# Layer 2's frequency products with the spectra stationary, its weights put in order of use by copies in memory, and layer 1 woven

## The chip, the cores and the metric

One core of a Trainium2 chip runs the whole program. The metric is the device time of one execution in microseconds (us), as the median of several; a smaller number is better. Next to the times stands the profile of one execution, which names the engines: PE (TensorE matmuls), PEld (its loads of stationary operands), DVE (VectorE), ACT (ScalarE), POOL (GpSimd) and SP, the engine whose queue (SPq) issues most transfers. PEclk is the share of full clock that TensorE was granted. "Issue" as the cause of idle time means that the engine waited for nothing that the profile shows. "The chain" is the work that ended last, followed back from each step to what released it. A matmul leaves two records in these traces (8448 for the 4224 of the products below).

## The reference

Four layers in float32 on x of 2 x 128 x 64 x 64, each of the form x = x + layer(group_norm(x)):

```python
# layer 0: 1x1 convolution to 5*128 channels, depth-wise 3x3, two attentions (4 heads), projection
# layer 1: a 1x3 convolution, correlations over 7 shifts, a 5x5 dilated depth-wise convolution
# layer 2: quaternion convolution by FFT
Xs = rfft2(x in 4 groups of 32 channels)                       # 64 x 33 frequencies
Ws = kr_{w,x,y,z} + 1j * ki_{w,x,y,z}                          # each 32 x 32 x 64 x 33
C  = einsum('piohw,qbihw->pqbohw', Ws, Xs)                     # 4 x 4 products per frequency
Pw = C[0,0] - C[1,1] - C[2,2] - C[3,3]                         # ... Px, Py, Pz: other signs and pairs
o  = irfft2(P)
# layer 3: attention with 8 heads of 16 channels over 4096 tokens
```

Each of the 64 x 33 frequencies of layer 2 has its own 128 x 32 complex matrix of weights (69 MB in all), and it meets only 2 images. This is what makes layer 2 awkward: many small products, each with weights of its own.

## The kernel before

Layers 0 and 3 (attention) are the long ones and stay almost as they are. Layer 2 has a way in (normalize, transform over h), the products with the transform over w (8 blocks of 4 rows and their 4 mirror rows, so 16 half blocks), and a way out. Its loads and products, and the order of steps in layer 1:

```python
wpool = ctx.enter_context(tc.tile_pool(name="l2_w", bufs=5))
def rows_of_weights(kb, mirror):          # one half block: 4 rows of 33 frequencies
    for part in "ri":
        wt = wpool.tile([128, 32, NF], F32, tag="w", name=f"w_{part}")
        for p in range(4):                # runs of 4 * 33 values, 528 bytes, in DRAM
            ...
            nc.sync.dma_start(wt[32 * p : 32 * p + 32, :, at:],
                array[:, :, r0 : lo + 4, :].rearrange("i o h w -> i o (h w)"))
# spectra of one row: a matmul against a sign-and-place matrix, then the transform over w
def transposed(i):
    nc.tensor.matmul(pt, y[:, b, m, :, :]..., k["perm"], start=True, stop=True)   # 512 columns
    nc.scalar.copy(yt, pt)
def transformed(i, yt):
    for r in range(0, 4, 2): ...          # 4 matmuls of 198 columns a row and image, DVE copies to e
def products(ws, e, got):
    for fw in range(FW):                  # 33 frequencies
        for n in range(2):                # real and imaginary weights
            for s in range(4):            # 4 rows, one column group of PE each
                nc.tensor.matmul(out...,  # stationary: weights, 128 x 32; moving: 16 columns
                    ws[n][:, :, s * FW + fw],
                    e[:, s, :, :, 1 - n : 3 - n, fw]..., start=(n == 0), stop=(n == 1))
# layer 1
g = [padded(0)]; prepared(); g.append(padded(1))
xt = [columns(g[0])]; t2 = [convolved(g[0])]; xt.append(columns(g[1]))
t3 = [correlated(xt[0])]; t2.append(convolved(g[1])); t3.append(correlated(xt[1]))
some(taps(0, g[0]), 42)                   # DVE: 42 taps of the depth-wise convolution, image 0
```

## Time and profile before

| | before |
|---|---|
| median of 3 runs (a fourth came with the result) | 4674.4 us (4664.9 to 4683.0) |
| profiled span, granted clock | 4670.5 us, 0.932 |
| layer 0 ends at | 1687.1 us |
| layer 1 | 302.8 us |
| layer 2: way in, products, way out | 45.2, 539.9, 78.9 us |
| layer 3: first to last exp | 1946.5 us |

### The profile page before, as it was taken

The numbers are of one execution on the slowest core, as the hardware profiler recorded it, in microseconds if no ns is written. First come the engines' busy times: TensorE is split into PE (matmuls) and PEld (weight loads), VectorE is DVE, ScalarE is ACT, GpSimd is POOL, SyncE is SP. The second block draws the span as 40 slices with busy tenths as digits, with TensorE's granted clock in tenths as the row PEclk, the third lists the DMA queues.
The fourth block names the chain that finished last, engine by engine and source line by source line (L and its number), as shares of the span: only waits on it lengthen the run. The fifth ranks groups of instructions, "written<-read, shape, count | busy, mean of one in ns | idle before, by whom it ended". The sixth has DMA issues, their size and how long they took to land.

```text
span 4670.5 us, 95822 instructions
## 1 busy us (share of the span) xinstructions
PE 4291.4 (92%) x42698; PEld 1787.4 (38%) x42698; DVE 2118.5 (45%) x2192; ACT 3264.9 (70%) x3735; POOL 59.3 (1%) x141
## 2 busy tenths in 40 slices
PE   6899999889999968976677889999999999999998
PEld 3522222452222234465556733333333333333332
DVE  3689999458999986951111221131113211221111
ACT  3478888437888821221111289999999999999998
POOL 1001000000000010000000000000000000000000
PEclk9999999999999979986676589999999999999999
DMA  1000000000000000088876000000000000000000
GB/s 44 2 1 1 1 1 1 1 2 1 1 1 1 1 6 1 1 136 130 129 119 95 7 3 6 6 5 4 6 6 6 6 6 6 6 6 6 6 6 4
DMA packets 154267, 90.60 MB, mean 19 GB/s; under 512 B 24297, under 2 KB 148201, under 8 KB 153842
## 3 DMA queue, kind: packets, MB, share of 16 engines
q1 hardware_dynamic: 153842, 84.36, 11.1%
q8 instruction: 337, 5.52, 0.5%
q14 instruction: 88, 0.72, 0.1%
HBM read 75.94 MB, written 4.19 MB: 17 GB/s over the span
## 4 chain that ended last, share of the span: by engine, by line
PE 85%; DVE 6%; issue 4%; ACT 3%; POOL 1%; DMA 0%; SPq 0%; DVEq 0%; ACTq 0%; POOLq 0%
PE ps_acc L1884 22%; PE ps_s L1865 18%; PE ps_s L1166 12%; PE ps_acc L1570 11%; PE ps_sp L1361 3%; PE ps_freq L875 3%; PE ps_bank L673 2%; PE ps_pe L842 2%; PE ps_bank L819 1%; DVE sums L1605 1%; PE ps_t L605 1%; PE ps_sp L1339 1%; PE ps_po L994 1%; PE ps_bank L590 1%; PE ps_bank L644 1%
## 5 line engine op out<-in xcount | busy, mean ns | idle before, releaser
L1875 ACT ACTIVATE weights<-ps_s 128x1024 f32<-128x1024 f32 x2048 | 1887.6, 1094 | 60.0 <-PE ps_s L1865 57.3
L1175 ACT ACTIVATE weights<-ps_s 128x1024 f32<-128x1024 f32 x1024 | 992.7, 1022 | 176.4 <-PE ps_s L1166 151.5
L1884 PE MATMUL ps_acc<-weights,vt 128*32 128x512 f32 x8192 | 1092.1, 605 | 0.0
L1865 PE MATMUL ps_s<-q,k 32*128 32x512 f32 x8192 | 931.3, 445 | 10.3 <-ACT weights L1875 10.3
L1605 DVE TENSOR_TENSOR sums<-sums,weights 128x2048 f32<-128x2048 f32 x384 | 879.1, 2289 | 44.6 <-ACT weights L1175 8.8
L1865 PEld LDWEIGHTS ps_s<-q,k 32*128 32x128 f32 x8192 | 473.2, 182 | 847.7 <-ACT weights L1875 788.8
L1166 PE MATMUL ps_s<-q,k 32*128 32x512 f32 x4096 | 648.1, 643 | 2.7 <-ACT weights L1175 1.3
L1570 PE MATMUL ps_acc<-weights,vt 128*32 128x512 f32 x4096 | 550.3, 607 | 3.4 <-ACT used L1595 3.2
L1906 DVE COPY u<-ps_acc 128x512 f32<-128x512 f32 x32 | 22.1, 692 | 1067.4 <-PE ps_acc L1884 1067.4
L1166 PEld LDWEIGHTS ps_s<-q,k 32*128 32x128 f32 x4096 | 210.1, 184 | 431.2 <-issue 215.4
L1884 PEld LDWEIGHTS ps_acc<-weights,vt 128*32 128x32 f32 x8192 | 163.0, 108 | 378.0 <-issue 366.0
L1570 PEld LDWEIGHTS ps_acc<-weights,vt 128*32 128x32 f32 x4096 | 81.1, 108 | 396.6 <-issue 378.4
L875 PE MATMUL ps_freq<-e,w_i 128*32 128x16 f32 x4224 | 141.1, 220 | 72.6 <-issue 72.6
L875 PE MATMUL ps_freq<-e,w_r 128*32 128x16 f32 x4224 | 143.1, 220 | 68.0 <-issue 67.5
L625 DVE SCALAR_TENSOR_TENSOR X<-g,w,X 128x2048 f32<-128x2048 f32 x84 | 197.3, 2350 | 2.4
L1361 PE MATMUL ps_sp<-pad,diag 32*32 32x512 f32 x4608 | 168.3, 611 | 6.1 <-DVE q L1372 4.8
L1605 DVE TENSOR_TENSOR sums<-weights 128x2048 f32<-128x2048 f32 x64 | 146.5, 2289 | 60.6 <-ACT weights L1175 60.6
L875 PEld LDWEIGHTS ps_freq<-e,w_i 128*32 128x32 f32 x4224 | 134.0, 159 | 76.6 <-issue 76.5
L875 PEld LDWEIGHTS ps_freq<-e,w_r 128*32 128x32 f32 x4224 | 134.7, 159 | 74.6 <-issue 73.6
L885 ACT COPY pz<-ps_freq 128x272 f32<-128x272 f32 x16 | 6.8, 423 | 211.2 <-PE ps_freq L875 211.2
L1826 DVE TENSOR_TENSOR vt<-ps_acc,bv 128x384 f32<-128x384 f32 x32 | 17.8, 557 | 292.1 <-PE ps_acc L1819 292.1
L885 DVE COPY pz<-ps_freq 128x256 f32<-128x256 f32 x16 | 6.8, 425 | 278.3 <-PE ps_freq L875 208.7
(278 smaller groups left out, 3196.9 us busy)
## 6 DMA issues: line engine op xcount, KB each, us to landing
w_r<-in_L_conv_kr_w SPq DMA_DIRECT2D x15, 528.0 KB, 12.3
w_r<-in_L_conv_kr_x SPq DMA_DIRECT2D x15, 528.0 KB
w_r<-in_L_conv_kr_y SPq DMA_DIRECT2D x15, 528.0 KB, 11.8
w_r<-in_L_conv_kr_z SPq DMA_DIRECT2D x15, 528.0 KB, 11.7
w_i<-in_L_conv_ki_w SPq DMA_DIRECT2D x15, 528.0 KB, 6.1
w_i<-in_L_conv_ki_x SPq DMA_DIRECT2D x15, 528.0 KB, 8.4
w_i<-in_L_conv_ki_y SPq DMA_DIRECT2D x15, 528.0 KB, 11.1
w_i<-in_L_conv_ki_z SPq DMA_DIRECT2D x15, 528.0 KB, 12.6
```

What stands on the lines that cost most here:

```text
L625: nc.vector.scalar_tensor_tensor(xi, g[:, i : i + H // 2, j : j + W], w8[:, s : s + 1], xi, ALU.mult, ALU.add)
L673: nc.tensor.matmul(ps.rearrange("p (h w) -> p h w", w=W), t9[:, k, :], t2[:, c * ROWS + k : (c + 1) * ROWS + k, 2 : W + 2], start=(k == 0) ...
L842: nc.tensor.matmul(pe[:, j * 6 * FW : j * 6 * FW + n * 3 * FW], yt[:, (r + j) * 128 : (r + j + 1) * 128], fwd_w[:, : n * 3 * FW], start=Tr ...
L875: nc.tensor.matmul(out.rearrange("p (x c) -> p x c", c=2), ws[n][:, :, s * FW + fw], e[:, s, :, :, 1 - n : 3 - n, fw].rearrange("p r b e - ...
L1166: nc.tensor.matmul(ps[j // 2][:, j % 2, :], k[rows, kt * 128 : (kt + 1) * 128], q[rows, qb * CH : (qb + 1) * CH], start=True, stop=True,)
L1175: nc.scalar.activation(w[:, 2 * p : 2 * p + 2, :], ps[p], AF.Exp)
L1361: nc.tensor.matmul(ps[r // 2][to, r % 2, :].rearrange("p (h w) -> p h w", w=W), diag[rows, grp, t, :], pad[rows, y0 : y0 + ROWS, t % 3 : t ...
L1570: nc.tensor.matmul(ac[n][rows, :], lhs(rows), w[:, j, :], start=first, stop=last)
L1605: nc.vector.tensor_add(parts[0].rearrange("p j c -> p (j c)"), t.rearrange("p j c -> p (j c)"), w.rearrange("p j c -> p (j c)"),)
L1865: nc.tensor.matmul(ps[j // 2][:, j % 2, :], k[rows, kt * 128 : (kt + 1) * 128], q[n][rows, qb * CH : (qb + 1) * CH], start=(n == 0), stop= ...
L1875: nc.scalar.activation(w[p], ps[p], AF.Exp)
L1884: nc.tensor.matmul(ac[0][32 * j : 32 * j + 32, :], vt[:, kt, j // 2, i : i + 2, :].rearrange("p a d -> p (a d)"), w[j // 2][:, i, :], star ...
```

## The change

Intent: fewer, larger instructions on PE in layer 2, loads in long runs, and less waiting at the seams. Its parts are

1. copies from memory to memory during layer 0 that put layer 2's weights into 32 tiles in order of use, 16.9 KB a partition in one run;
2. products with the spectra stationary and the weights of two frequencies moving (128 columns): 68 matmuls a half block in place of 264. The result now has the frequencies' values in the wrong axis, so DVE transposes 32 x 32 blocks and combines them. The sign-and-place matmul gives way to small signed copies, half on ACT and half on DVE;
3. layer 1 with columns and convolution woven into each other;
4. group norm statistics of a layer taken in the last steps of the layer before; in layer 2 the normalizing goes from DVE to ACT.

The core of the diff (cut; renamed constants, the fallback path and small reorderings in layer 0 are left out):

```diff
+def _weights_by_rows(nc, pool, a):                       # called at the start of layer 0
+    for kb ...: for mirror ...: for part in "ri":
+                t = pool.tile([128, 32, NF], F32, tag=name, name=name)     # pool in DRAM
+                for p in range(4):
+                    nc.sync.dma_start(t[32 * p : 32 * p + 32, :, at:],
+                        array[:, :, r0 : lo + 4, :].rearrange("i o h w -> i o (h w)"))
 ...
-    wpool = ctx.enter_context(tc.tile_pool(name="l2_w", bufs=5))
+    wpool = ctx.enter_context(tc.tile_pool(name="l2_w", bufs=2))
+        ws = wpool.tile([128, 2, 32, NF], F32, tag="w", name="w_ri")
+        for n, part in enumerate("ri"):
+            nc.sync.dma_start(ws[:, n], weights[kb, mirror, part])
 ...
+            def copied(r, p, n=1):                       # within placed(), a row and image
+                out = e[to, row, :, 4 * r : 4 * r + 4].rearrange("p f (b c) -> p b f c", c=2)
+                if scalar: nc.scalar.mul(out, got[of, :, s], sign)
+                else:      nc.vector.tensor_scalar_mul(out, got[of, :, s], sign)
+            copied(0, 0, 4); copied(2, 2, 2); copied(2, 0); copied(2, 1)
+            for r in (1, 3):
+                for p in range(4): copied(r, p)
 ...
+            for j in range(PAIRS):                       # 17 pairs of frequencies
+                for s in range(4):
+                    w = ws[:, :, :, fw : fw + 2]         # neighbours 528 bytes apart in o
+                    nc.tensor.matmul(out.rearrange("p (n f o) -> p n f o", n=2, f=2),
+                        e[:, s, 2 * j : 2 * j + 2, :].rearrange("p f x -> p (f x)"),
+                        w.rearrange("p n o f -> p n f o"), start=True, stop=True)
+                if j % 4 == 3 or last: nc.vector.transpose(zf[:, lo : lo + n], ph[:, :n])
+            for c in range(2): nc.vector.tensor_tensor(pz[..., c]..., *parts, ADD or SUBTRACT)
 ...
-    xt = [columns(g[0])]; t2 = [convolved(g[0])]; xt.append(columns(g[1])) ...
+    xt, t2 = zip(*(columns_and_convolved(x) for x in g))
+    t3 = [correlated(x) for x in xt]
 ...
+                for i in stats: next(i)                  # in layer 0's finish: layer 1's statistics
```

## The prediction

> **What bounds the kernel now.** I read the slices of the page first: they separate the layers.
>
> ```profile
> PE   6899999889999968976677889999999999999998
> ...
> PEclk9999999999999979986676589999999999999999
> DMA  1000000000000000088876000000000000000000
> ```
>
> A slice is 117 us. DMA works in five slices only, 17 to 21, and there alone PE falls to 6 or 7 tenths and the granted clock to 6 or 5. That is layer 2. Everything else is PE (attention of layers 0 and 3), which the change leaves alone. Next, the busy time by stage, cut at the instructions that begin and end each one (columns: stretch, its length, busy us with instruction counts of PE, PEld, DVE, ACT, POOL, then clock, DMA share, GB/s).
>
> ```profile
> 1702.00:1732.00 30.00, 10.07 (x37) 7.11 (x38) 27.96 (x35) 12.54 (x16) 0.00 (x0) 0.50 0.00 0
> 1755.00:1777.00 22.00, 8.36 (x34) 5.60 (x34) 21.72 (x10) 12.95 (x17) 0.00 (x0) 0.63 0.00 0
> 1992.00:2037.00 45.00, 33.15 (x203) 28.10 (x204) 39.93 (x88) 12.54 (x35) 0.00 (x0) 0.81 1.23 194
> 2037.00:2571.00 534.00, 381.41 (x9475) 323.39 (x9474) 99.04 (x288) 64.01 (x114) 0.00 (x0) 0.69 0.77 116
> 2571.00:2656.00 85.00, 82.30 (x400) 78.66 (x399) 16.13 (x38) 18.65 (x32) 1.67 (x7) 0.50 0.01 2
> ```
>
> Layer 1 runs from 1688 to 1990; two of its stretches leave PE two thirds idle. Layer 2 has a way in (to 2037), the products (534 us, 67 us for each of 8 blocks of rows) and a way out (85 us, PE full at half clock). In the products DVE and ACT are nearly free. So I asked who waits there, for engines and for the DMA queue:
>
> ```profile
> PEld ps_freq L875 <- issue: 150.1, 73, 6.5
> PE ps_freq L875 <- issue: 140.2, 54, 6.4
> ```
>
> ```profile
> SPq L749 <- PE ps_freq L875: 224.3, 13, 22.8
> ```
>
> PE loses 140 us to "issue", nothing visible, in gaps of about 6 us; no wait for weights appears at all. The DMA queue on its side waits for PE to give buffers back. 381 busy and 140 idle are 521 of the 534: PE is the bound, with holes. The order of time shows their shape:
>
> ```profile
> 2127.65 6.21 issue
> 2133.86 2.21 PE ps_freq L875 x110
> ```
>
> A burst of 110 to 124 matmul records in 2.2 us, then 6.2 us of nothing, again and again while DMA runs at 1.24 of its 16 engines. With a weight load each, a burst is near 256 instructions; the page's instruction queue (q8: 337 packets, 5.52 MB) moves 16.4 KB a packet, 256 instructions of 64 B. So PE is starved of instructions by the weight traffic: 8.4 us for a block of them.
>
> **The Trainium skill.** "Runtime: NRT & Kernel Launch", section Instruction fetch mechanics: instructions arrive in 16 KiB blocks of 256 over a DMA queue of the sequencer. The packet size and burst length agree; its remark that the refill is hidden does not hold here. "DMA: Bandwidth & Descriptors", section Queues, rings and completion order: an SDMA engine serves its queues in turn, a packet at a time, which fits. "TensorE: Matmul & The Clock Gate", Part 1: the clock is half or full by recent activity, and Part 4 says transposes do not count as activity. The way out, all transposes and 64-column matmuls, was granted 0.50 with PE busy 82 of 85 us, which agrees. Part 3 there says that matmuls on different column groups overlap: the attention's chain has pieces of 24 records (three times four 32-wide matmuls of 512 columns) in 3.07 us, 1.02 us a four, where a single full one takes 0.87 (24 in 20.8 us in layer 1), so it holds.
>
> **The change part by part.**
>
> *Copies in layer 0.* 16 half blocks of 8 x 528 KB, 69 MB, go from memory to memory into tiles with 16.9 KB a partition. The old loads of the same 528-byte runs reached 190 GB/s when unhindered (the 1992 row), so at least 364 us, from about 15 us on, against 1940 us until they are needed: no wait for them. Cost: instruction fetch in the first convolutions (45 to 222 us, 5123 PE and PEld instructions, 20 blocks, one per 8.9 us against 8.4). It is borderline; I charge **+15 us**. Attention (8838 in 618 us, a block per 18 us) is safe.
>
> *Layer 1.* The statistics move into layer 0's last step (16 more of 0.68 us on a DVE that had 22 of 36 us there, so that step grows by about 7, as much as the start of layer 1 saves). Dense PE work thus still starts near 1702. Then columns and convolution are woven: per image 24 matmuls (20.8 us from the 1807 piece) and 32 transposes (about 8) are 29 us, twice 58; correlations 57 as now. 115 us in place of 155 (1702 to 1857). DVE's 42 taps (99 us) end by about 1810, just ahead. The last 133 us are PE-bound and stay. **-38 us**, taking 2 us for seams.
>
> *Layer 2, way in.* The first statistics (10 us, 1990 to 2000) are done in layer 1, normalizing moves from DVE to ACT, a copy the other way. DVE per step 0.37+0.61, with the second statistics 37 us in all; PE 33 to 38. **-8 us**.
>
> *Products*, per block of rows. Instructions: before 528 matmuls (two records each) plus 8 of 512 columns (6.8 us), 32 of 198 (12) and the turning back. Now 136 matmuls of 128 columns, four at a time. From the 1.02 us for 512 columns, 0.25 us a four: 34 x 0.25 = 8.5 us. The sign matrix falls away: 8 transposes and 8 matmuls of 136 columns, about 4.5; turning (3.8) and back (3.5) stay. **PE 20 us** at full clock, 40 at half. PE instructions drop to some 740, 2.9 blocks: 24 us at 8.4.
> The signs go to copies: 4 rows x 2 images x 12 = 96 of 136 elements, half each. **DVE**: 48 x 0.265 (0.327 a 198-element copy, less 62 elements at 1.04 ns) = 12.7; 8 transposes of 512 at the 0.74 of a shuffle, 2 small ones, 4 combinations (0.43), 2 copies (0.69): **22 us**. **ACT**: 48 x about 0.34, 4 x 0.37, 4 x 0.58: **20 us**. **DMA**: 8.65 MB; input rows of 4 KB moved at 386 GB/s (window 5 to 10 us), so **22 us**.
> Four engines near 20 to 24 us, so none gives slack: two weight buffers (a half block refilled only after its products end), in-order engines, two PSUM banks a tag. With the clock at today's 0.69 PE takes 29. I choose 33 us a block: 7 x 33 + 28 for the last + 10 before + 6 after = 275 against 534: **-259 us**.
>
> *Way out and layer 3.* Same code at half clock, 85 us. Its statistics for layer 3 save about 8 of the 50 us before attention begins: **-8 us**.
>
> Sum: +15 - 38 - 8 - 259 - 8 = -298; 4674 - 298 = 4376, say **4375 us**.
>
> **The rivals.** (1) The fetch starvation just moves: into layer 0, where conv bursts of 288 records in 9.7 us outrun a block per 8.4 us, or stays in layer 2 under denser DMA. For: bursts today stall within two blocks, so little is stocked ahead. Against: the average demand is just met. If memory-to-memory traffic slows fetches by half: +60, 4435. (2) Small copies become the bound: 96 with semaphores and strided writes may cost 0.4 us each and serialize with PE through the two banks; 45 us a block, 4470. For: 12 per row are a chain. Against: two engines share them. (3) PE falls to half clock, because transposes weigh more: 40 us a block, 4430. (4) All overlaps well: 25 us a block, 4305. (5) The loads were hidden anyway, and only issue gaps vanish: the 140 us plus the 38 of layer 1, 4490.
>
> **Range and chances.** Rivals 1 to 3 may add up in part; rival 4 sets the other end: 4285 to 4470. Even rival 5 is 4% faster; slower by 2% would need layer 0 to lose 390 us. Faster 0.96, same 0.03, slower 0.01.
>
> **What would show it.** Right: issue waits on the products fall from 140 us to under 30; the products span 240 to 310 us; DVE and ACT are each busy over 60% of it; DMA moves 250 GB/s or more while it loads; the way out is still 85 us at 0.50; dense work from the start of layer 1 to its end shrinks by about 38. Wrong: layer 0 ends more than 40 us later with issue gaps in the convolutions, DMA still filling the first 1000 us; PE waiting for copies for over half of a block; a weight load ending a wait of PE.

## More of the kernel before

The stages are cut at the starts of instructions: layer 0 ends with its last addition to X, layer 1 likewise, the way in with its last copy to y, the way out runs from its first transpose to its last addition. They differ by a few us from the rounded windows of the prediction. One view more than the prediction shows, the groups of instructions in the products, with the costliest of them. The columns are line, engine, operation, out<-in, shapes, count; then busy us and mean ns of one; then the idle time just before them and what ended it.

```profile
L875 PE MATMUL ps_freq<-e,w_r 128*32 128x16 f32 x4224 | 143.1, 220 | 68.0 <-issue 67.5 <-DVE e L851 0.5
```

A matmul with only 16 moving columns still has a record of 220 ns, and there are 2 x 4224 records of them (real and imaginary weights).

## The result and the profile after

| | before | after |
|---|---|---|
| median (runs) | 4670.8 us (4) | 4385.3 us (4), 4377.1 to 4392.2 |
| profiled span, granted clock | 4670.5 us, 0.932 | 4375.3 us, 0.968 |
| layer 0 ends at | 1687.1 us | 1699.5 us |
| layer 1 | 302.8 us | 261.9 us |
| layer 2: way in, products, way out | 45.2, 539.9, 78.9 us | 37.9, 279.6, 80.3 us |
| end of way out to first exp of layer 3 | 52.7 us | 48.4 us |
| layer 3: first to last exp | 1946.5 us | 1951.1 us |

The ratio is 0.9385 (95% interval 0.9359 to 0.9411): the results are correct and the kernel is faster. The ratios are not quite the ratios of the medians.

The same three rows of slices as before (here a slice is 109 us):

```profile
PE   6899999979999997988887999999999999999998
...
PEclk9999999999999999999985999999999999999999
...
DMA  9996000000000000004640000000000000000000
```

DMA works in the first four slices, where the copies now run, and in three slices, 18 to 20 (counted from 0, as in the prediction), where it was busy in five. The slices with PEclk 5 or 6 in the middle of layer 2 are gone; the way out is still the low one. The busy time by stage, columns as in the prediction (the DMA share is the summed time of packets over 16 engines' time, so it can pass 1; the 1.24 of the prediction is all engines full, not 1.24 of them):

```profile
1720.00:1780.00 60.00, 60.00 (x180) 28.81 (x179) 59.15 (x26) 26.55 (x39) 0.00 (x0) 1.00 0.00 1
1963.00:2001.00 38.00, 32.16 (x201) 26.45 (x201) 31.50 (x77) 24.95 (x34) 0.55 (x1) 0.91 0.56 234
2001.00:2278.00 277.00, 230.77 (x2778) 145.88 (x2778) 187.51 (x501) 144.47 (x464) 0.00 (x0) 0.93 0.56 220
2278.00:2356.00 78.00, 77.24 (x376) 73.40 (x375) 19.39 (x45) 18.09 (x32) 0.55 (x1) 0.50 0.00 1
```

From 20 us after the start of layer 1 PE is busy all the time, where it had long stretches two thirds idle. In the products PE has 2778 records in place of 9475, a clock of 0.93 in place of 0.69, and DVE and ACT work beside it. Who waits in the products, for engines and for the queue:

```profile
PE ps_bank L1004 <- DVE pz L992: 22.7, 13, 2.9
...
PEld ps_z L975 <- issue: 12.7, 50, 1.0
...
PE ps_z L975 <- DMA w_ri<-w_i: 2.8, 2, 2.2
```

```profile
SPq L789 <- PE ps_bank L975: 251.1, 14, 52.0
```

The 140 us of PE in "issue" at the products are gone: what is left of it is 12.7 us on the weight-load side, in pieces of 1 us at most. PE's new wait is for DVE's combinations (pz); for the loaded weights it waits 2.8 us in all, while the loads wait 251 us for PE to free a buffer, not the other way round. In order of time a stretch of a block reads:

```profile
2144.20 0.30 DVE e L916
2144.53 0.33 DVE z L984
2144.88 1.16 DVE pz L992 x2
2146.18 1.04 PE ps_bank L1004 x4
2147.22 1.06 PE ps_z L975 x16
```

This is the new form of the bound: DVE's copies, transposes and combinations end, then PE turns the result and goes on with the next products. Of this chain over one block, PE's products have 24%, DVE's copies 24%, its transposes 12% and its combinations 10%. The groups that matter:

```profile
L975 PE MATMUL ps_z<-w_ri,e 128*32 128x128 f32 x2048 | 138.1, 407 | 10.3 <-DVE e L916 5.3 <-DMA w_ri<-w_i 2.8 <-ACT e L914 2.1
L914 ACT ACTIVATE e<-ps_pe 32x136 f32<-32x136 f32 x330 | 92.7, 281 | 3.9
L916 DVE TENSOR_SCALAR e<-ps_pe 32x136 f32<-32x136 f32 x310 | 92.0, 297 | 4.3
...
L992 DVE TENSOR_TENSOR pz<-z 128x272 f32<-128x272 f32 x32 | 18.3, 655 | 0.5
```

One block takes 33.0 us (a stretch of 32.9 us in the middle: PE 27.6 us, DVE 23.9, ACT 17.6, DMA share 0.67, 263 GB/s).

### The profile page after: what moved, and what is told of

Read it like the earlier page. It is cut to its first block, busy times and chain, and to the rows that moved or that the text cites. A ratio compares the mean times of both kernels' runs of the same rounds, so it can differ in the third digit from the quotient of the medians.

```text
span 4375.3 us, 82819 instructions
## 1 busy us (share of the span) xinstructions
PE 4128.4 (94%) x35988; PEld 1595.2 (36%) x35988; DVE 2203.8 (50%) x2410; ACT 3353.7 (77%) x4080; POOL 68.0 (2%) x145
## 4 chain that ended last, share of the span: by engine, by line
PE 82%; DVE 13%; ACT 3%; issue 1%; POOL 0%; DMA 0%; SPq 0%; DVEq 0%; ACTq 0%; POOLq 0%
PE ps_acc L2057 23%; PE ps_s L2038 19%; PE ps_s L1313 13%; PE ps_acc L1726 12%; DVE X L649 4%; PE ps_sp L1517 4%; PE ps_z L975 2%; DVE sums L1761 1%; DVE e L916 1%; PE ps_po L1130 1%; PE ps_sp L1495 1%; PE ps_acc L1992 1%; ACT weights L1322 1%; PE ps_pt L1117 1%; PE ps_acc L1966 1%
## 5 line engine op out<-in xcount | busy, mean ns | idle before, releaser
L975 PE MATMUL ps_z<-w_ri,e 128*32 128x128 f32 x2048 | 138.1, 407 | 10.3 <-DVE e L916 5.3
L1517 PEld LDWEIGHTS ps_sp<-pad,diag 32*32 32x32 f32 x4608 | 93.5, 104 | 77.6 <-issue 32.5
L1495 PE MATMUL ps_sp<-xn,w_qkv 128*128 128x512 f32 x160 | 89.2, 695 | 32.6 <-DVE k L1528 15.2
L2082 DVE RECIPROCAL r<-r 128x512 f32<-128x512 f32 x32 | 107.3, 3353 | 1.1
L914 ACT ACTIVATE e<-ps_pe 32x136 f32<-32x136 f32 (+1 forms) x363 | 102.0, 281 | 4.2
L916 DVE TENSOR_SCALAR e<-ps_pe 32x136 f32<-32x136 f32 (+1 forms) x341 | 101.1, 297 | 4.7
## 6 DMA issues: line engine op xcount, KB each, us to landing
w_r<-in_L_conv_kr_w SPq DMA_DIRECT2D x15, 528.0 KB, 12.4
w_i<-in_L_conv_ki_w SPq DMA_DIRECT2D x15, 528.0 KB, 12.4
```

Source lines behind the costliest of these rows:

```text
L916: nc.vector.tensor_scalar_mul(out, got[of, :, s], sign)
L975: nc.tensor.matmul(out.rearrange("p (n f o) -> p n f o", n=2, f=2), e[:, s, 2 * j : 2 * j + 2, :].rearrange("p f x -> p (f x)"), w.rearran ...
L1495: nc.tensor.matmul(ps[:, i // ROWS, : rows * W], w_qkv[:, grp * C : (grp + 1) * C], xn[:, (first + r0 + i) * W : (first + r0 + i + rows) * W],
L1517: nc.tensor.matmul(ps[r // 2][to, r % 2, :].rearrange("p (h w) -> p h w", w=W), diag[rows, grp, t, :], pad[rows, y0 : y0 + ROWS, t % 3 : t ...
```

## The experiments

Twelve kernels ran, in three sets of four, each set on one chip with its own runs of the kernel before (medians 4672.0, 4675.4 and 4677.5 us). One execution of each was profiled. How far a stage repeats is seen where nothing in it changed: the products took 279.6, 279.3, 279.2 and 279.1 us in four kernels that share them. Layer 0's end does not repeat so well while copies run in it: it fell between 1699.3 and 1710.3 us in ten kernels that have the copies at its start. Whole times of two variants therefore differ by some us for that reason alone, and small differences are read from stages.

### The two halves of layer 2's change, one at a time: direct_loads and before_copies

direct_loads is the changed kernel without the copies:

```diff
-        for n, part in enumerate("ri"):
-            nc.sync.dma_start(ws[:, n], weights[kb, mirror, part])
+        for n, part in enumerate("ri"):
+            for p in range(4): ...   # the old loads from the input, runs of 528 bytes
-    rows_of_weights = _weights_by_rows(nc, dram, a)
+    rows_of_weights = a
```

> The changed kernel without the copies: layer 2 loads its weights straight from the inputs in runs of 528 bytes, as before. Theory A (the copies pay because long rows move faster): a half block of 4.3 MB at 190 GB/s takes 22.8 us, two of them 45 us a block of rows against 33 measured, so the products grow from 278 us to about 375, the waits of PE there are waits for a weight load, and layer 0 gets back about 4 us: about 4480 in all. Rival B (the number of PE instructions mattered, not how the weights come): the products stay within 20 us of 278 and the whole near 4385. Rival C (short packets starve the instruction fetch again): products over 375 with issue waits of PE over 50 us on them.

Measured: correct, 4467.2 us, ratio 0.9565 (0.9549 to 0.9581); products 378.3 us. Layer 0 ends at 1687.5 us. The products' longest wait of PE, and their busy times:

```profile
PE ps_z L985 <- DMA w_ri<-in_L_conv_ki_z: 118.4, 14, 13.2
```

```profile
1989.00:2366.00 377.00, 237.19 (x2782) 152.27 (x2782) 188.38 (x502) 145.10 (x465) 0.00 (x0) 0.81 1.09 167
```

With the new products but the old loads PE waits for the loads, 118 us in pieces of up to 13 us, and the mean DMA share is 1.09. The 69 MB at the 190 GB/s that such loads reached in the kernel before (the way in, in the prediction) are 364 us; the products take 378. So the loads of 528-byte runs would have become the bound. It is also seen here that the reordering and the statistics in layer 0 cost nothing in sum: without copies it ends where it did before (1687.1), its first exp 6 us sooner.

before_copies is the kernel before, with the copies in layer 0 and its loads from them:

```diff
+    rows_of_weights = _weights_by_rows(nc, dram, a)      # in layer 0 of the kernel before
-            for p in range(4): ...                       # loads from the input
+            nc.sync.dma_start(wt, weights[kb, mirror, part])
```

> The kernel before, with the copies of layer 0 alone added; its products still load the same five weight buffers, now in rows of 16.9 KB. Theory A (the 140 us of issue gaps come from DMA engines kept full by short runs): DMA is full for 11 us of each 20 instead of 22 of 27, gaps fall to about 50 us, products from 534 to about 440, the whole to about 4590. Rival (any weight traffic of the same bytes starves the fetch as much): gaps stay over 110 us and the whole stays within 30 us of 4671.

Measured: correct, 4597.6 us, ratio 0.9838 (0.9821 to 0.9854); products 454.3 us; layer 0 ends at 1699.3 us. Waits in its products:

```profile
PEld ps_freq L889 <- issue: 109.0, 172, 4.1
...
PE ps_freq L889 <- issue: 39.8, 23, 4.0
```

and busy times:

```profile
2046.00:2500.00 454.00, 409.38 (x9492) 328.01 (x9492) 100.38 (x291) 63.07 (x114) 0.00 (x0) 0.83 0.34 131
```

PE's time in "issue" falls from 140 to 40 us with the same number of PE instructions. Its busy time rose by 28 us (381 to 409), so the gain is smaller than the gaps that went. What changed is only the traffic beside it: the DMA share over the products went from 0.77 to 0.34, because the weights now come in long runs. So the gaps of "issue" did come from the traffic of short runs, though gaps of up to 4 us stay.

That they are waits for instructions can be read from the traces, which record the packets of the instruction queue (q8) with their times. In the products of the kernel before, PE and its weight loads stand still together for over 1.5 us 36 times, 119 us in all. In each of the 36 just one q8 packet of 16,384 bytes lands, and PE goes on 1.2 to 1.8 us after that. (The gap that the prediction shows, 2127.65 to 2133.86 us, has one that lands at 2132.65.) The 9 such gaps of before_copies are alike (29 us, 1.3 to 1.6 us after a landing); in the 11 of the changed kernel none lands. direct_loads has the short runs too, but its products take 22 such packets in place of 75, and PE has one issue wait of 6.1 us on them: its rival C is refuted, and most of the 140 us took both, many instructions and short runs. In the 12 gaps over 4 us the packet starts only 2.2 to 3.6 us into the gap; why it starts late is not shown beyond its going with the short runs.

Together: new instructions alone give 162 us in the products, copies alone 86, both 260. The sum of the single gains is 248, so they nearly add, and neither is enough: one leaves the loads as the bound, the other the instructions.

### Are the loads hidden in the changed kernel? no_loads

```diff
+        if kb:
+            return kept[mirror]        # after the first block: the first block's weights again
```

> The changed kernel with the weights of the first block of rows used for all eight (wrong results on purpose), so that no weight load runs during the products. Theory (loads are hidden now and PE with its seams is the bound): products fall by no more than 8 us from 278 (the trace shows 3 us of waits for a load and some 13 us of issue waits on the products). Rival (loads or starved fetches still slow every stage): they fall by over 20 us.

Measured: wrong (relative error 0.39), 4374.0 us, ratio 0.9358 (0.9343 to 0.9374); products 278.5 us against 279.6. The loads cost nothing: with copies in order of use, two buffers are enough.

### What makes a product slow? contiguous and pairs

The prediction had taken 0.25 us for four products side by side (one to each column group, each with its own 32 stationary columns); the trace shows 1.03 to 1.06 us for 16 records, two fours, so some 0.5 us a four. In the changed kernel a moving operand takes one value of every 528 bytes. contiguous lets it read 128 values that lie side by side (wrong ones):

```diff
-                        w = ws[:, :, :, fw : fw + 2]
-                        w.rearrange("p n o f -> p n f o"),
+                    w = ws.rearrange("p n o f -> p (n o f)")[:, at : at + 128]
+                        w,
```

> The changed kernel with the moving operand of the products read as 128 neighbouring elements instead of single elements 528 bytes apart (wrong results on purpose, the same number of instructions and elements). Measured now: four products, one to each column group, take 0.46 to 0.5 us where 0.25 was predicted. Theory S (the stride halves the read): a four falls to about 0.27 us, PE busy falls by some 7 us of 28 a block, the block from 33 us to about 28, the products to about 240. Rival F (a fixed cost of short matmuls, or only two column groups at once): a four stays at 0.46 and nothing moves by more than 3 us.

Measured: wrong (0.41), 4372.4 us, ratio 0.9361 (0.9345 to 0.9376); products 272.5 us. pairs, run later, keeps the right values but reads the two frequencies' values next to each other, 8 bytes at a time, and lets the matmul write them apart in PSUM:

```diff
-                        out.rearrange("p (n f o) -> p n f o", n=2, f=2),
-                        w.rearrange("p n o f -> p n f o"),
+                        out.rearrange("p (n f o) -> p n o f", n=2, f=2),
+                        w,
```

> Results correct. The moving weights of two frequencies are read in the order in which they lie (part, output channel, frequency), so two neighbouring values at a time: 64 jumps of 528 bytes in a matmul in place of 128; the matmul's result is written to PSUM in the old order, with strides there. If each jump costs, a product's record falls from 407 ns about half way to the 273 ns of the contiguous run, to some 340 ns, PE's busy time a block from 28 to 26 us, and the products from 280 to about 276 us: whole near 4372, ratio 0.936, hardly to be told from the changed kernel in time, but plain in the records. Rival: any read that isn't contiguous costs as much (records stay at 407 ns), or the strided write takes the gain back.

Measured: correct, 4378.1 us, ratio 0.9363 (0.9343 to 0.9384); products 272.6 us, PE busy 208.7 us of them against 230.8. The records of the products, first of the changed kernel, then of contiguous, then of pairs (smallest, median and largest ns of one, after the colon):

```profile
L975 PE MATMUL ps_z<-w_ri,e x2048: 386/408/434, 2007.8 to 2269.5; 128*32 128x128 f32 x187
```

```profile
L973 PE MATMUL ps_z<-w_ri,e x2048: 272/273/423, 2010.8 to 2265.5; 128*32 128x128 f32 x187
```

```profile
L975 PE MATMUL ps_z<-w_ri,e x2048: 273/300/445, 2011.9 to 2266.5; 128*32 128x128 f32 x187
```

Single values 528 bytes apart make a record half as long again as values side by side (408 against 273 ns); pairs of values take back four fifths of that (300). The expectation of half way was wrong in the good direction. (The 273 that later expectations quote for contiguous is this median; its mean is 315, with records of up to 423 ns at a mean clock of 0.82.) But the products gained only 7 us of the 22 that PE was busy less in pairs, and of 36 in contiguous. Where did the rest go? In contiguous the wait for DVE's combinations rose:

```profile
PE ps_bank L1002 <- DVE pz L990: 35.2, 15, 3.1
```

from 22.7 us, and the granted clock fell from 0.93 to 0.82. PE alone isn't the bound.

### Is DVE the other half of the bound? wide_copies and wide_contiguous

wide_copies makes 4 copies of 128 partitions a row and image in place of 12 small ones, which puts values in the wrong place but does the same number of elements:

```diff
+                of = to if n == 4 else ...       # no change of place: the wrong results
-            copied(2, 2, 2); copied(2, 0); copied(2, 1)
+            copied(2, 0, 4)
             for r in (1, 3):
-                for p in range(4): copied(r, p)
+                copied(r, 0, 4)
```

> WRONG RESULTS on purpose: the signed copies of spectra are 4 a row and image, 128 partitions wide and without the change of place, in place of 12 (10 small of 32 partitions, one of 64, one of 128). This takes about 64 copies of some 0.29 us out of a block, half from VectorE, half from ScalarE: about 9 us of each engine's 24 and 18 a block. If the copies on VectorE share the bound with PE (28 of 33 us a block), PE is left to bind: a block of 28 to 30 us, products about 245 us in place of 280, the whole near 4345, ratio 0.930. If copies alone bind: blocks near 24 us, products 200. If PE with its loads of weights alone binds: products within 8 us of 280.

> WRONG RESULTS on purpose: both the wide copies and moving weights that lie side by side. Side by side weights alone took the matmul records from 407 to 273 ns and PE's busy time from 28 to 24 us a block, but the products only from 280 to 273 us. If PE and VectorE bind in turn, both edits together give more than their sum alone: blocks of about 22 us, where the loads' rate (8.65 MB at 260 to 390 GB/s, 22 to 33 us a block) begins to bind: products 190 to 220 us, the whole near 4310, ratio 0.923, and waits of PE for the loaded weights appear. If something else binds (the chain through the two banks), products stay over 240 us.

Measured: wide_copies, wrong (0.36), 4353.0 us, ratio 0.9312 (0.9297 to 0.9328), products 245.8 us. wide_contiguous, wrong (0.41), 4303.9 us, ratio 0.9212 (0.9192 to 0.9233), products 196.5 us. Busy time in the products, wide_copies first:

```profile
2008.00:2252.00 244.00, 221.10 (x2778) 139.46 (x2778) 110.96 (x254) 67.95 (x201) 0.00 (x0) 0.98 0.63 250
```

```profile
2005.00:2200.00 195.00, 166.18 (x2779) 127.66 (x2780) 108.62 (x254) 68.34 (x200) 0.00 (x0) 0.94 0.76 313
```

Faster products alone give 7 us, fewer copies alone 34, both together 83. Two causes of which each hides the other: with wide copies PE is busy 221 of 244 us, and only then the faster products count. (PE waits there for loaded weights too, 10.2 us, and loads have 22% of the chain over its products, so they are near to counting.) The transfers are no limit up to 313 GB/s in this last run. Both runs cut ACT's copies too, so they do not tell DVE's part from ACT's; the chain of the changed kernel over all its products, where DVE's small copies have 22% and ACT's 4%, speaks for DVE, but that is a reading.

### Can copies be saved correctly? fewer_copies

```diff
-            copied(2, 0)
-            copied(2, 1)
+            copied(2, 0, 2)                         # one copy of 64 partitions, a column of signs
-                if scalar:
+                if scalar or (r == 3 and p > 1):    # two copies a row go from DVE to ACT
```

> Results correct. Two of the 12 signed copies a row and image become one of 64 partitions with a column of signs (88 in place of 96 a block), and two more of those on VectorE go to ScalarE: VectorE 36 and ScalarE 52 copies a block in place of 48 each. By the durations of the trace VectorE goes from 23.9 to about 20.3 us a block and ScalarE from 17.6 to 18.7. If VectorE's copies are the half of the bound that wide_copies showed (9 us less on VectorE, 34 us less for the products), this gives a third of that: products about 268 us in place of 280, whole near 4365, ratio 0.934. Rival: ScalarE's copies matter as much, or the order in which they are done: products within 4 us of 280.

Measured: correct, 4381.6 us, ratio 0.9361 (0.9345 to 0.9378); products 275.0 us, between the theory's 268 and its rival. DVE fell to 165 us and ACT rose to 158, as the durations said; but

```profile
L915 ACT ACTIVATE e<-ps_pe 32x136 f32<-32x136 f32 x326 | 91.4, 280 | 29.6 <-DVE e L917 25.7
```

ACT now idles 29.6 us before its small copies, 25.7 of it until a copy of DVE into the same tile has ended; it was 3.9 us in the changed kernel, where a row's copies were all of one engine. It reaches PE: its waits for DVE's combinations fell from 22.7 to 15.2 us, but those for ACT's copies of turned spectra (yt) rose from 8.6 to 17.3. Much of the gain became this. (Its whole time does not show the 5 us: its layer 0 ended at 1709.6.)

### Layer 1: unwoven

```diff
-    xt, t2 = zip(*(columns_and_convolved(x) for x in g))
-    t3 = [correlated(x) for x in xt]
+    xt = [columns(g[0])]; t2 = [convolved(g[0])]; xt.append(columns(g[1]))     # the old order
+    t3 = [correlated(xt[0])]; t2.append(convolved(g[1])); t3.append(correlated(xt[1]))
```

> Results correct. Layer 1 has its columns and its convolutions apart again, in the old order of steps; the early statistics and everything else of the change stay. If the weaving is what shortened layer 1 (prediction: 38 us, by dense PE work of 115 us in place of 155), layer 1 goes from 262 back to about 297 us and the whole to about 4410 us, ratio 0.944. Rival: most of the 41 us came from the statistics that moved into layer 0's last step (16 steps of about 0.7 us, and the chain behind them), so layer 1 stays under 280 us and the whole under 4395.

Measured: correct, 4422.6 us, ratio 0.946 (0.9444 to 0.9476); layer 1 takes 299.8 us against 261.9. So the weaving is worth 38 us, and the statistics that moved out of layer 1 some 3. The chain shows why. First some pieces of unwoven, then the wait that they cause (here in the kernel before: us in total, times, longest), then DVE's taps in the changed kernel:

```profile
1735.14 21.97 PE ps_bank L611 x48
1779.16 28.84 PE ps_t L626 x64
1809.10 20.79 PE ps_bank L611 x48
1829.88 27.48 PE ps_t L626 x64
```

```profile
DVE t L663 <- PE ps_bank L616: 41.0, 1, 41.0
```

```profile
L649 DVE SCALAR_TENSOR_TENSOR X<-g,w,X x84: 2340/2352/2354, 1716.5 to 1938.0; 128x2048 f32<-128x2048 f32 x84
```

Unwoven, PE's convolutions and correlations stand one after another on the chain until 1857 us, as before the change. DVE has then long finished the 42 taps of the first image and waits for them, 37.7 us (41.0 in the kernel before), until it can go on to the second image. Woven, no such wait is left, and that is the gain. 74% of layer 1's chain are now DVE's 84 taps, 2.35 us each, from 1716 almost without a gap to 1940 us; DVE is busy 239 of 262 us. PE is off most of the chain, but it is busy 244 us itself.

### Copies that start later: late_copies

A tiny transfer from a result of the first image's convolutions is put ahead of each copy of a tile:

```diff
-    rows_of_weights = _weights_by_rows(nc, dram, a)
+        if b == 0:                                # after convolutions(pool, 0, ...)
+            rows_of_weights = _weights_by_rows(nc, dram, a, own[:, 0, 0:1])
+                if after is not None:             # in _weights_by_rows, before the copies
+                    nc.sync.dma_start(t[:, 0, 0:1], after)
```

> Results correct. The copies of the weights start only when the convolutions of layer 0's first image have ended (each copy's tile is first touched by a tiny transfer that needs their result). If the copies cost time because they crowd out PE's instructions in those convolutions, the first exp of layer 0's attention comes at about 220 us (229 in the changed kernel, 219 without copies), layer 0 ends near 1690 us (1699.5), and the whole is about 10 us faster than the changed kernel: near 4365 us, ratio to before 0.935. Rival: the 12 us come from elsewhere in layer 0 (the new order of its last step, or the copies beside attention or beside the second image's convolutions): then layer 0 still ends near 1700 and the whole stays near 4376.

Measured: correct, 4368.8 us, ratio 0.9345 (0.9329 to 0.936); layer 0 ends at 1690.8 us. The exps of layer 0's attention (first and last start), of the changed kernel and of late_copies:

```profile
L1322 ACT ACTIVATE weights<-ps_s x1024: 1002/1023/1059, 229.0 to 1652.0; 128x1024 f32<-128x1024 f32 x171
```

```profile
L1324 ACT ACTIVATE weights<-ps_s x1024: 1002/1023/1058, 218.7 to 1643.3; 128x1024 f32<-128x1024 f32 x171
```

The first exp comes 10 us sooner, and the gain is still there at the end. Beside attention the same copies cost little (layer 0 ends 3 us after that of direct_loads, which has none). The wait that the copies caused is in the trace of the first convolutions: the changed kernel's weight loads of the depth-wise matmuls wait

```profile
PEld ps_sp L1517 <- issue: 23.4, 48, 3.1
```

for "issue", against 10.2 us in the kernel before and 7.0 in late_copies. The instruction packets agree: between 45 us and the first exp the changed kernel has 6 gaps of PE (9.1 us in all) that end 1.1 to 1.9 us after such a packet lands, the kernel before, direct_loads and late_copies none.

### The start of layer 3: l3_early

```diff
+    early_tiles, ready = early(one)       # in layer 2: loads of layer 3's constants and weights
+        ready()                           # before the way out: scales them
-    k3 = _load_consts(nc, one, src, 2) ...
+    upper, sign, lower, w_qk, b_qk, w_v, b_v = early
```

> Results correct. Layer 3's constants and weights are loaded during layer 2 into memory that layer 2 doesn't use, and scaled there before the way out. If the 7.3 us in which PE waits after the last addition of the way out are the wait for these loads, it falls to about 1 us, first exp of layer 3 comes 41 to 43 us after the end of layer 2 (48.4 in the changed kernel), and the whole is 6 to 7 us faster: near 4370, ratio 0.935. Rival: another chain (VectorE's folding, the sums of POOL) takes the place of the wait, and first exp still comes 46 us or more after the end of layer 2.

Measured: correct, 4376.3 us, ratio 0.9351 (0.9332 to 0.937). From the timeline of the changed kernel, then of l3_early (start, us, engine, line, operation; idle time before and its end in brackets):

```profile
2362.44 0.30 DVE L1915 TENSOR_SCALAR w_qk<-w 128x64 f32<-128x64 f32 x2 [2.82 <-DMA b_qk<-in_L_conv_bq]
...
2366.46 0.98 PE L1941 MATMUL ps_acc<-st,wqk 128*128 128x1 f32 x4 [7.31 <-DVE wqk L1932]
```

```profile
2369.26 0.98 PE L1948 MATMUL ps_acc<-st,wqk 128*128 128x1 f32 x4 [1.11 <-DVE wqk L1939]
```

PE's wait falls from 7.3 to 1.1 us and the first exp comes 43.8 us after the end of layer 2, just over the 41 to 43 expected, in place of 48.4 (48.4 to 50.2 in the nine experiments that leave the changed layer 3 as it is). The whole time does not tell it from the changed kernel, since its layer 0 ended 11 us later (1710.3).

### The four correct parts together: best

late_copies, pairs, fewer_copies and l3_early in one kernel.

> Results correct. The changed kernel with late copies, pairs, fewer copies and layer 3's early loads together. If the parts add (10, 4, 12 and 6 us), the whole is near 4345 us, ratio 0.930, below both kernels: layer 0 ends near 1690, products 262 to 268 us, first exp of layer 3 some 42 us after the end of layer 2. If pairs and fewer copies relieve PE and VectorE together, the products may gain more than the sum, as the run with both wrong edits did (83 us against 7 and 34): 255 us, whole near 4335.

Measured: correct, 4356.5 us (4354.1 to 4358.6, 5 runs), ratio 0.9308 (0.9294 to 0.9322). It beats the kernel before and the changed kernel (0.9359 to 0.9411). Layer 0 ends at 1690.6 us and the first exp of layer 3 comes 43.5 us after layer 2, as expected. The products take 275.3 us, not the 255 to 268 expected: pairs alone had 272.6. PE was busy 219 of 273 us there at a clock of 0.87 (209 of 270 at 0.91 in pairs), and ACT waited 26 us for DVE's copies as in fewer_copies. Against pairs, PE waited 16 us less for DVE but 14 us more for ACT. So the copies given to ACT seem to take back what they relieve DVE of; no run leaves them on DVE, so this stays open.

## Why the prediction was right

It said 4375 us with 4285 to 4470; the median is 4385. In terms of the profiled spans, by its own steps:

| step | predicted | measured |
|---|---|---|
| layer 0, copies | +15 | +12.4 |
| layer 1 | -38 | -40.9 |
| way in | -8 | -7.3 |
| products | -259 | -260.3 |
| way out | 0 | +1.4 |
| start of layer 3 | -8 | -4.3, then +3.8 in the rest of layer 3 |
| sum | -298 | -295.2 |

**The bound before** was read rightly. Issue gaps come with the traffic of short runs: before_copies took 100 of the 140 us away without touching an instruction of PE, and the packets of the instruction queue land in the gaps.

**Copies in layer 0.** The mechanism and the size were right: 12 us here, up to 23 in other kernels with these copies, and 3 when they wait for the convolutions to end. Rival 1, 60 us more, did not come. That it could be avoided was not seen.

**Layer 1.** The size was right and shown by unwoven. The step "the last 133 us are PE-bound and stay" was not: once woven, DVE's taps run from 1716 to 1940 us and set the end, with a PE tail of 20 us. The first image's 42 taps begin no earlier (1714 us before, 1716 now); the second image's do, since DVE no longer waits 41 us for PE. The next gain has to relieve DVE, and PE with it, which is busy 244 of the 262 us.

**Products.** 33 us a block was chosen, not derived, from four engines near 20 to 24 us without slack, and the block takes 33.0. The terms behind it were less good, and two errors cancelled:

- "0.25 us a four: 34 x 0.25 = 8.5 us" failed. The products' records keep PE busy 149 us, 18.6 a block. The step took the time from contiguous moving operands of the attention; here the moving values lie 528 bytes apart. The Trainium skill has the reason to look for: "SBUF — State Buffer", section Door 1: The DMA port swizzle, says that SBUF is read in lines of 16 bytes, wants two hits a line, and charges a crossing. The runs fit: single values 408 ns, pairs 300, side by side 273; none tells lines of 16 bytes from the mere number of places. It was not looked up for a matmul's operand.
- "With the clock at today's 0.69 PE takes 29" failed as well: the clock granted was 0.93 (0.83 in before_copies, where 40 of the 140 us of gaps were left). With slower products but a better clock PE is busy some 28 us a block, near the 29 by luck.
- DVE at 22 us a block was near (23.9): the combination cost 0.655 us each, not 0.43, and a small copy 0.297, not 0.265: the 0.327 that the step began from was the pace in a row of four (1.31 us), the record of one copy is 0.362, and the same step from it gives 0.298. ACT was 17.6, not 20.
- "None gives slack" was the right idea, and the runs prove it: 7, 34 and 83 us for faster products, fewer copies, both. Rival 4 (25 us a block, if all overlaps well) is what wide_contiguous reaches, 24.6 on average, with wrong results.

**Signs named beforehand.** Right: issue waits on the products under 30 us, products within 240 to 310, DMA over 250 GB/s while loading (263 in a block), way out at 0.50 (whether its transposes or its short matmuls hold the clock there no run tells). Half wrong: DVE was busy 68% of the products, but ACT only 52%, where over 60% was named for both. Of the signs of being wrong one came in small: a weight load ended two waits of PE, 2.8 us in all; no_loads shows that this cost next to nothing.

**The way in** came as predicted (-7.3 us); no run tests its cause.

**The start of layer 3** is another step that failed. The statistics are gone from it as the step said, but only 4.3 of the 8 us came (2.5 to 4.3 in the other kernels with it): the loads of layer 3's weights, which had run behind the statistics, are issued only when the last addition of layer 2 has freed their memory, and PE waits 7.3 us. l3_early shows it by taking it away. The 4.6 us by which the attention of layer 3 got longer are not explained; the experiments have 1945 to 1953 us there, before_copies with the old layer 3 among them (1952.7), so most of it may be scatter.

**Rival 5** (loads hidden anyway, only the gaps vanish) is refuted: direct_loads has the products at 378 us, with 118 us of waits for loads. (Its 4490 should read 4496 by its own terms.)

## What to carry to other kernels

When many small matmuls stall in "issue", look at what traffic runs beside them, and cut both: here fewer instructions or longer runs alone gave 162 or 86 us, both 260. It is worth giving a moving operand at least two neighbouring float32 values at every place it touches, and writing the result apart in PSUM rather than reading apart in SBUF: a record fell from 408 to 300 ns here. When two engines share a bound, remove one cost at a time by a wrong-on-purpose kernel and also both together: each alone may show next to nothing.

## What the Trainium skill lacked or had wrong

- "Runtime: NRT & Kernel Launch", section Instruction fetch mechanics, calls the cost of crossing from one block of instructions to the next mostly hidden. Here PE lost 140 us to "issue" beside DMA of short runs and 40 us beside long ones, in gaps of which each over 1.5 us ends 1.2 to 1.8 us after a 16 KB packet of the instruction queue lands. The page lacks what traffic does to the fetch.
- "SBUF — State Buffer", section Door 1: The DMA port swizzle, also says that any access to PSUM that isn't contiguous slows matmuls significantly. pairs writes PSUM with a stride of 32 values and reads SBUF by twos, and its median record is 300 ns against 273 with both contiguous: at most a tenth. The page gives no figure for its line crossings; for float32 moving values 528 bytes apart a 128-column record took 408 ns.
- "DMA: Bandwidth & Descriptors", section Latency and other measured facts, gives up to 214 GB/s for copies between tensors in HBM with rows of 16 KiB. Here copies in runs of 528 bytes moved at 191 and 192 GB/s in the second and third slices, so they lost little; what no page gives is their cost to the computing beside them, 12 to 23 us.
- No page gives the time of small float32 matmuls on four column groups with strided operands: a four of 128 columns took some 0.5 us with values 528 bytes apart and 0.29 us at best with values side by side (16 records in 0.57 us).
